# The beginning of a graph kernel: weights loaded ahead of the adjacency, and the start's steps in another order

## The chip, the cores and the metric

The kernel runs on one core of a Trainium2 chip. The core has five engines with an instruction queue each: TensorE (PE, matrix products), VectorE (DVE), ScalarE (ACT), GpSimd (POOL) and SyncE (SP, which here only issues transfers). Each runs its queue in order, and waits on semaphores for the others. The metric is the device time of one execution in microseconds (us), median of several runs. "The profile" is one execution recorded by the hardware profiler. Its own time is given beside its span, the time from its first to its last instruction.

## The reference

128 independent graphs of 128 nodes with 64 features; `adj` is 128 x 128 for each graph, about one entry in eight is positive.

```python
mask = (adj > 0.0)
h  = relu(layernorm(x))
# layer 0: for each edge j-k a hidden row of 192
hid[j,k] = relu(h[j] @ W1a + (h[j] - h[k]) @ W1b + b1)
x1 = x + sum_k(mask[j,k] * hid[j,k]) @ W2 + deg[j] * b2
# layer 1: plain aggregation
out = x1 + (adj @ relu(layernorm(x1))) @ W.T
```

## The kernel before, in words

The graphs are taken in 32 groups of four. For each group the kernel loads `x` and `adj`, normalises `x` into `h`, turns it on TensorE (`hT`), and turns `adj` (`adj_pe`, `adj_act`) to make `maskT`. A product with the weights `wp` gives `pp` (`pp_pe`): for each node its part as the edge's start, its part as the edge's end, and a third block of 64 columns. A second product, a row of ones times `biasp`, adds the bias to `pp`. The projections are then cut into three bf16 parts that add up to the f32 value, called `ca` (`pp_ca`, `pp_rest`, `pp_second`, `pp_third`: first part, what is left, second part, third part). Twelve transfers (`stack`, tile `k`) put these parts under each other so that one matmul sums them.

The edges are found by rank. A product of `maskT` with a triangular matrix counts the edges of each node within each quarter of its neighbours. Comparing these ranks with 0 to 5 gives one-hot rows `S`. In group 0 this is done by `first_ranks` (matmul into `pk`, ScalarE copy to `q`) and `first_slots(0, q)` (six VectorE comparisons for quarter q, four quarters), and in later groups by `rank_pe`, `rank_act` and `slot`. `over` and `count_pe`/`count_dve` count edges beyond six in a quarter, and yield the degrees and the scale `ns` that `pp_z` and the degree column `dn` that `pp_e` need.

The main work of a group is 24 jobs (`Job`). `fill` multiplies `S` and `k` into one of three PSUM buffers `g`; `drain` reduces it on VectorE (tile `hm`, two thirds of the jobs) or on ScalarE and GpSimd (tile `T`). TensorE can fill three jobs ahead; the fourth needs a drained buffer. After the jobs come the second layer and the output.

Before group 0 the weights are prepared. `weight_loads` issues W1 on SyncE's queue and four small loads on ScalarE's. `weights_a` halves W2 (`w2h`) and spreads b1. `weights_b` adds the halves of W1 (`wab`, into `wp`), turns the sum, and copies it to `wT`; `weights_b2` multiplies `wT` by `w2h` into `pc`, copies that to `wp`, and adds `b2s` to the product `pbw` to complete `bias`. `weights_c(i)`, i = 0 to 2, splits `bias` into three bf16 parts, three VectorE steps for each part but the last, which has two: a cast (`bp`), the part's share of `biasp`, and the remainder (`br`).

What sets the order: the class `Engine` (its calls all appear as L198 in the profile) holds VectorE, ScalarE, GpSimd and SyncE to the written order during the beginning and in groups 1 to 30; matmuls (L181) and transposes (L184) always keep the written order. Group 0's jobs and the steps of `PLAN0` beside them are left to the scheduler. Two things outside the written lines matter. A transfer carries one of eight semaphores in turn, so an issue also waits until the transfer eight before it in that count has landed. And `buffer` hands out PSUM buffers in turn (three `g`, two `m`), so a step can wait for the last reader of its buffer. `keep_busy` issues matmuls whose result nobody reads; TensorE has them between group 0's counts and its jobs.

The beginning is written as calls from `load(0)` (L1119) to `Engine.held = False`.

Of the kernel before, what the change touches and what calls it, by code (L numbers as in the profile page):

```python
# [150 lines left out]
def kernel(  # L151
# [28 lines left out]
    def mm(*args, **kw):  # L180
        return tc.keep_in_program_order(nc.tensor.matmul(*args, **kw))  # L181

    def tp(*args, **kw):
        return tc.keep_in_program_order(nc.tensor.transpose(*args, **kw))  # L184
# [43 lines left out]
    with ExitStack() as main:  # L228
# [16 lines left out]
        def gtile(name, key=None):  # L245
            i = buffer("g", key, 3)
            return ps_g.tile([P, 2, 512], F32, tag=f"g{i}", name=name)

        def mtile(name, key=None):
            i = buffer("m", key, 2)  # L250
            return ps_m.tile([P, 512], F32, tag=f"m{i}", name=name)
# [54 lines left out]
        def constants():  # L306
            vec.tensor_scalar(ioe, iov, BIG, None, ALU.add)
            vec.tensor_reduce(
                id32, ident.rearrange("p (q j) -> p j q", q=Q), AX.X, ALU.add
            )  # L310
            vec.tensor_copy(id3, id32)

        def constants2():
            vec.tensor_copy(identb, ident)
            vec.tensor_copy(upb, upper)
# [12 lines left out]
        def weight_loads():  # L328
            act.dma_start(w2a, W2[0:C0, :])
            act.dma_start(b1c, b1[0:C0].unsqueeze(1))  # L330
            act.dma_start(bias[:, 0:H], b1.unsqueeze(0).to_broadcast([P, H]))
            act.dma_start(b2s, b2.unsqueeze(0).to_broadcast([P, O]))
            for p in range(2):
                s = slice(p * F, (p + 1) * F)
                sp.dma_start(w1[s], W1.rearrange("(t f) h -> f t h", t=2))

        def weight_loads2():
            for p in range(2):
                s = slice(p * F, (p + 1) * F)
                sp.dma_start(w2bd[s, p, :], W2[C0:H, :])  # L340
                sp.dma_start(wl1[s, s], W)
# [8 lines left out]
            vec.tensor_copy(b1x, b1c.to_broadcast([P, P]))  # L350

        def weights_b():
            pbw = gtile("pbw")
            mm(pbw[:, 0, 0:O], b1x, w2h, start=True, stop=True)
            vec.tensor_tensor(wab, w1[:, 0], w1[:, 1], ALU.add)
            tp(pbw[:, 1, 0:P], wab[:, 0:C0], ident)
            vec.tensor_scalar(wp[:, 0:H], w1[:, 1], -1.0, None, ALU.mult)
            vec.tensor_copy(wT, pbw[:, 1, 0:P])
            return pbw

        def weights_b2(pbw):
            pc = mtile("pc")
            mm(pc[:, 0:O], wT, w2h, start=True, stop=True)
            vec.tensor_copy(wp[:, 2 * H : 2 * H + O], pc[:, 0:O])
            vec.tensor_tensor(bias[:, H : H + O], pbw[:, 0, 0:O], b2s, ALU.add)

        left = [bias]

        def weights_c(i):
            pt = one.tile([P, H + O], BF16, tag=f"bp{i}", name=f"bp{i}")  # L370
            vec.tensor_copy(pt, left[i])
            if i == 0:
                vec.tensor_scalar(biasp, pt, id64[:, i : i + 1], None, ALU.mult)
            else:
                vec.scalar_tensor_tensor(
                    biasp, pt, id64[:, i : i + 1], biasp, ALU.mult, ALU.add
                )
            if i < 2:
                left.append(one.tile([P, H + O], F32, tag=f"br{i}", name=f"br{i}"))
                vec.tensor_tensor(left[i + 1], left[i], pt, ALU.subtract)  # L380
# [3 lines left out]
            tp(pl[:, 0:P], wl1, ident)  # L384
            vec.tensor_copy(wl1t, pl[:, 0:P])

        groups: dict[int, dict] = {}

        def bc(t, n, axis):
            shape = list(t.shape)  # L390
# [4 lines left out]
        def norm_a(src, u):  # L395
            st = tmp.tile([P, G, 6], F32, tag="st", name=f"st{u}")
            mv = tmp.tile([P, G, 2], F32, tag="mv", name=f"mv{u}")
            for b in range(G):
                vec.bn_stats(st[:, b, :], src[:, b, :])
            for b in range(G):  # L400
                vec.bn_aggr(mv[:, b, :], st[:, b, :])
            return mv
# [36 lines left out]
        def stats_a(g):  # L439
            d = groups[g]  # L440
            d["mv"] = norm_a(d["x"], f"a{g}")
# [22 lines left out]
            d = groups[g]  # L464
            normed(d["h2"][:, b, :], d["x1"], d["scales"], b)

        def load(g):
            d = groups[g] = {}
            d["x"] = loads.tile([P, G, F], F32, tag="x", name=f"x{g}", bufs=3)
            sp.dma_start(d["x"], x[g * G : (g + 1) * G].rearrange("b n f -> n b f"))  # L470
            d["adj"] = loads.tile([P, G, N], F32, tag="adj", name=f"adj{g}")
            sp.dma_start(d["adj"], adj[g * G : (g + 1) * G].rearrange("b j k -> j b k"))

        def keep_busy(tile, n):
            for _ in range(n):
# [2 lines left out]
        def adj_pe(g):  # L478
            d = groups[g]
            pt = d["pt"] = mtile(f"pt{g}", "adj_pe")  # L480
            for b in range(G):
                tp(pt[:, b * N : (b + 1) * N], d["adj"][:, b, :], ident)

        def adj_act(g):
            d = groups[g]
            d["adjT"] = grp.tile([P, G, N], F32, tag="adjT", name=f"adjT{g}", bufs=4)
            act.activation(
                d["adjT"].rearrange("k b j -> k (b j)"), d["pt"], AF.Copy
            )
# [12 lines left out]
        def rank_pe(g):  # L502
            d = groups[g]
            d["pq"] = mtile(f"pq{g}", "rank_pe")
            mm(
                d["pq"], triq, d["maskT"].rearrange("k b j -> k (b j)"), start=True, stop=True
            )
# [28 lines left out]
                        d["S"][q * QN : (q + 1) * QN],  # L536
                    )

        def first_ranks(g, qp):

            d = groups[g]
            pk = gtile(f"pk{g}_{qp}")
            if qp == 0:
                d["q3"] = tmp.tile([K3, Q, G * N], BF16, tag="T", name=f"q3{g}", bufs=3)
            for i in range(2):
                q = 2 * qp + i
                mm(
                    pk[0:K3, i], triq3[:, q].rearrange("k t j -> k (t j)"),
                    d["maskT"].rearrange("k b j -> k (b j)"), start=True, stop=True,
                )  # L550
            act.activation(d["q3"][:, 2 * qp : 2 * qp + 2], pk[0:K3], AF.Copy)

        def first_slots(g, q):

# [8 lines left out]
        def hT_pe(g):  # L563
            d = groups[g]
            ph = d["ph"] = mtile(f"ph{g}", "hT_pe")
            for r in range(2):
                tp(
                    ph[:, r * N : (r + 1) * N],
                    d["h"][:, r].rearrange("n p f -> n (p f)"),
                    ident,  # L570
                )

        def hT_act(g):
            d = groups[g]
            d["hT"] = tmp.tile([P, 2, N], F32, tag="hT", name=f"hT{g}", bufs=1)
            act.activation(
                d["hT"].rearrange("p r n -> p (r n)"), d["ph"][:, 0 : 2 * N], AF.Copy
            )
# [59 lines left out]
        def pp_ca(g, r):  # L638
            act.activation(part(g, r, 0), both(g, r), AF.Copy)
# [35 lines left out]
        def pre_proj(g, r, between=None):  # L675
            pp_pe(g, r, between)
            pp_ca(g, r)
            return (
                lambda: pp_rest(g, r), lambda: pp_z(g, r), lambda: pp_e(g, r),
                lambda: pp_second(g, r), lambda *engines: pp_third(g, r, engines),  # L680
            )
# [434 lines left out]
        ORDERL += c0s[12:]  # L1116


        load(0)  # L1119
        weight_loads()  # L1120
        groups[0]["mv"] = norm_a(groups[0]["x"], "a0")
        constants2()
        groups[0]["scales"] = norm_s(groups[0]["mv"], "a0")
        weights_a()
        constants()
        adj_pe(0)
        pre_norm(0)
        adj_act(0)
        pb = weights_b()
        load(1)  # L1130
        weight_loads2()
        hT_pe(0)
        hT_act(0)
        weights_b2(pb)
        mask(0)
        for i in range(3):
            weights_c(i)
        steps = [pre_proj(0, 0, lambda: first_ranks(0, 0))]
        first_slots(0, 0)
        steps[0][0]()  # L1140
        steps += [pre_proj(0, 1, lambda: (rank_pe(0), rank_act(0), over(0)))]
        (residual, zs, es, second, third), (residual1, zs1, es1, second1, third1) = steps
        residual1()
        count_pe(0)
        count_dve(0)
        second()
        second1()
        third(pool, pool)
        third1(vec, vec)
        stack(0)  # L1150
        first_slots(0, 1)
        adj_pe(1)
        adj_act(1)
        mask(1)
        stats_a(1)
        keep_busy(mtile("keep"), 14)
        zs()
        es()
        zs1()
        es1()  # L1160
        first_ranks(0, 1)
        first_slots(0, 2)
        pre_norm(1)
        first_slots(0, 3)
        Engine.held = False
        ahead = {}

# [62 lines left out]
```

## Time and profile before

| what | us |
|---|---|
| time, median of 3 runs | 922.36 (919.47, 922.36, 926.63) |
| profiled execution, own time | 924.5 |
| its span | 922.7 |
| TensorE busy | 881.8 (96% of the span) |
| VectorE busy | 820.5 (89%) |
| ScalarE busy | 767.4 (83%) |
| GpSimd busy | 721.9 (78%) |
| mean granted TensorE clock | 0.984 of full |
| first job's matmuls start (`g`) | 24.45 |
| first `hm` reduction starts | 28.42 |

The first four rows compare executions: the profiled one lies 2.1 above the median of the three, which spread over 7.2. The busy shares are means over the whole span; TensorE's 96% says which engine limits the long middle, and nothing of the first 60 us, where every engine has gaps. The last two rows are positions in the span and mark where the beginning ends.

### The profile page before, as it was taken

What the parts mean: (1) busy time and instruction counts of PE and PEld (TensorE: products, weight loads), DVE (VectorE), ACT (ScalarE), POOL (GpSimd) and SP (SyncE); (2) the same over time, 40 slices, a digit from 0 to 9 for tenths busy, and PEclk for the clock granted to TensorE, in tenths of its full rate; (3) what the DMA queues carried; (4) which work ended last, traced back from release to release, by engine and by line L of the source; (5) the groups of instructions that cost most, each with busy time, mean ns of one, the idle gap of its engine ahead of it and who ended that gap; (6) DMA issues with size and microseconds to landing.
All of it is one profiled execution on the core that took longest, in us unless ns stands there. A gap on an engine that the chain in (4) does not pass through costs nothing.

```text
span 922.7 us, 26432 instructions
## 1 busy us (share of the span) xinstructions
PE 881.8 (96%) x9721; PEld 679.0 (74%) x9722; DVE 820.5 (89%) x2070; ACT 767.4 (83%) x1722; POOL 721.9 (78%) x1098
## 2 busy tenths in 40 slices
PE   5789999999999999999999999999999999999995
PEld 2467777777777777777777777777777777777774
DVE  6769999999999998899999999999999999999953
ACT  4659888889888888988888988888898888899841
POOL 1368888888888888788888888888888888888873
PEclk9799999999999999999999999999999999999997
DMA  3627666667666666766666766666676666577610
GB/s 91 133 70 160 156 151 141 141 144 178 151 155 149 142 140 157 162 155 154 141 140 141 179 155 152 147 140 141 157 167 155 156 144 138 142 169 162 137 25 15
DMA packets 88294, 129.88 MB, mean 141 GB/s; under 512 B 47200, under 2 KB 63968, under 8 KB 88160
## 3 DMA queue, kind: packets, MB, share of 16 engines
q1 hardware_dynamic: 87584, 127.98, 60.8%
q8 instruction: 78, 1.28, 0.6%
q14 instruction: 56, 0.46, 0.1%
q10 hardware_dynamic: 576, 0.16, 0.1%
HBM read 13.01 MB, written 4.19 MB: 19 GB/s over the span
## 4 chain that ended last, share of the span: by engine, by line
PE 80%; DVE 7%; POOL 5%; ACT 3%; DMA 2%; issue 2%; SPq 1%; DVEq 0%; POOLq 0%; ACTq 0%
PE g L181 45%; PE pp L181 7%; PE px L181 6%; PE pe L181 6%; PE py L181 5%; DVE hm L198 4%; POOL T L198 4%; PE po L181 2%; PE pj L181 2%; PE pt L184 2%; DMA k<-ca 1%; ACT T L198 1%; PE pga L181 1%; DVE S L198 1%; PE pd L181 1%
## 5 line engine op out<-in xcount | busy, mean ns | idle before, releaser
L198 POOL TENSOR_TENSOR T<-T 128x192 f32<-128x192 f32 (+2 forms) x768 | 524.1, 688 | 116.8 <-ACT T L198 72.1
L198 DVE TENSOR_REDUCE hm<-g 128x64 f32<-128x768 f32 x512 | 471.2, 951 | 44.3 <-PE g L181 44.0
L181 PEld LDWEIGHTS <-k 96*128 96x128 bf16 (+1 forms) x5544 | 362.1, 105 | 145.8 <-issue 55.9
L181 PE MATMUL g<-S,k 96*128 96x384 bf16 (+1 forms) x2048 | 373.4, 330 | 20.3 <-DVE hm L198 12.8
L181 PE MATMUL g<-id,k 96*64 96x192 bf16 (+1 forms) x3496 | 308.6, 247 | 0.0
L198 ACT ACTIVATE T<-g 128x768 f32<-128x768 f32 x256 | 197.5, 810 | 105.6 <-PE g L181 96.0
L198 POOL TENSOR_TENSOR ca<-rest,ca 128x384 bf16<-128x384 f32 x126 | 112.4, 912 | 59.4 <-ACT ca L198 44.8
L198 ACT ACTIVATE g<-at 128x768 f32<-128x768 f32 x150 | 120.4, 816 | 2.6 <-DVE hm L198 2.4
L198 DVE TENSOR_SCALAR S<-qs 128x512 bf16<-128x512 bf16 x186 | 88.5, 491 | 0.3 <-ACT qs L198 0.3
L181 PE MATMUL pe<-RT,X 128*64 128x128 f32 (+1 forms) x512 | 70.5, 280 | 0.0
L181 PE MATMUL pp<-wp,hT 64*128 64x448 f32 x256 | 67.5, 604 | 0.4 <-DVE bias L198 0.4
L198 ACT ACTIVATE z<-pp,ns 128x128 f32<-128x128 f32 (+1 forms) x256 | 66.6, 361 | 0.0
L198 DVE TENSOR_TENSOR rest<-pp,ca 128x768 f32<-128x768 f32 x64 | 60.6, 946 | 0.4 <-ACT ca L198 0.4
L198 ACT ACTIVATE h<-x,mra,rsa 128x64 f32<-128x64 f32 x128 | 56.9, 449 | 1.8 <-issue 1.3
L181 PEld LDWEIGHTS pe<-RT,X 128*64 128x64 f32 (+1 forms) x512 | 52.7, 165 | 5.5 <-issue 5.4
L198 ACT ACTIVATE ca<-rest 128x768 bf16<-128x768 f32 x64 | 53.9, 841 | 1.7 <-DVE rest L198 1.7
L181 PE MATMUL px<-ca,S 128*128 128x192 bf16 x384 | 53.2, 248 | 0.8 <-DVE S L198 0.8
L198 ACT ACTIVATE ca<-pp 128x768 bf16<-128x768 f32 x64 | 51.8, 810 | 1.6 <-PE pp L181 1.6
L181 PE MATMUL px<-ca,R 128*128 128x192 bf16 x384 | 53.2, 248 | 0.0
L181 PE MATMUL pe<-ident,z 128*128 128x128 f32 x192 | 49.1, 283 | 0.0
L198 POOL TENSOR_TENSOR hm<-T 128x64 f32<-128x64 f32 x128 | 41.1, 321 | 9.9
L198 ACT ACTIVATE et<-iov,mid 128x128 f32<-128x128 f32 x128 | 47.5, 399 | 0.0
(127 smaller groups left out, 1243.5 us busy)
## 6 DMA issues: line engine op xcount, KB each, us to landing
S<-S SPq DMA_DIRECT2D x372, 192.0 KB, 4.1
k<-ca SPq DMA_DIRECT2D x384, 96.0 KB, 2.2
adj<-in_adj_dram SPq DMA_DIRECT2D x32, 256.0 KB, 3.2
x<-in_x_dram SPq DMA_DIRECT2D x32, 128.0 KB, 2.6
out_dram<-ot SPq DMA_DIRECT2D x32, 128.0 KB, 2.2
w<-in_L_gnn_W_dram SPq DMA_DIRECT2D x2, 96.0 KB, 5.0
bias<-in_L_gnn_b_dram ACTq DMA_DIRECT2D x1, 96.0 KB, 4.1
w2a<-in_L_gnn_W_dram ACTq DMA_DIRECT2D x1, 32.0 KB, 2.2
```

What stands on the lines that cost most here:

```text
L181: return tc.keep_in_program_order(nc.tensor.matmul(*args, **kw))
L184: return tc.keep_in_program_order(nc.tensor.transpose(*args, **kw))
L198: ins = f(*args, **kw)
```

## The change

Only the beginning is rewritten; the jobs and `PLAN` are the same text. The lines that matter:

```diff
-            act.dma_start(bias[:, 0:H], b1.unsqueeze(0).to_broadcast([P, H]))
             act.dma_start(b2s, b2.unsqueeze(0).to_broadcast([P, O]))
+            act.dma_start(bias[:, 0:H], b1.unsqueeze(0).to_broadcast([P, H]))
...
-        load(0)
+        load_x(0)
         weight_loads()
+        load_adj(0)
         groups[0]["mv"] = norm_a(groups[0]["x"], "a0")
-        constants2()
         groups[0]["scales"] = norm_s(groups[0]["mv"], "a0")
         weights_a()
-        constants()
-        adj_pe(0)
         pre_norm(0)
-        adj_act(0)
         pb = weights_b()
         load(1)
         weight_loads2()
+        bias_b2(pb)
+        weights_b1(pb)
+        weights_c(0)
         hT_pe(0)
+        adj_pe(0)
         hT_act(0)
-        weights_b2(pb)
+        adj_act(0)
+        weights_b2()
         mask(0)
-        for i in range(3):
-            weights_c(i)
-        steps = [pre_proj(0, 0, lambda: first_ranks(0, 0))]
-        first_slots(0, 0)
-        steps[0][0]()
-        steps += [pre_proj(0, 1, lambda: (rank_pe(0), rank_act(0), over(0)))]
...
-        count_pe(0)
-        count_dve(0)
-        second()
-        second1()
-        third(pool, pool)
-        third1(vec, vec)
-        stack(0)
-        first_slots(0, 1)
-        adj_pe(1)
-        adj_act(1)
-        mask(1)
-        stats_a(1)
-        keep_busy(mtile("keep"), 14)
-        zs()
-        es()
-        zs1()
-        es1()
-        first_ranks(0, 1)
-        first_slots(0, 2)
-        pre_norm(1)
-        first_slots(0, 3)
+        weights_c(1)
+        weights_c(2)
+        pp_pe(0, 0, lambda: (turns.update(g=2), first_ranks_pe(0, 0)))
+        turns["g"] = 1
+        pp_pe(0, 1)
+        rank_pe(0)
+        pp_ca(0, 0)
+        pp_ca(0, 1)
+        pp_rest(0, 0)
+        pp_rest(0, 1)
+        pp_second(0, 0)
+        pp_second(0, 1)
+        pp_third(0, 0, (pool, pool))
+        pp_third(0, 1, (vec, vec))
+        rank_act(0)
+        first_ranks_act(0, 0)
+        stack(0)
+        over(0)
+        count_pe(0)
+        first_slots(0, 0)
+        count_dve(0)
+        first_slots(0, 1)
+        adj_pe(1)
+        keep_busy(mtile("keep"), 9)
+        for r in range(2):
+            pp_z(0, r)
+            pp_e(0, r)
+        adj_act(1)
+        turns["g"] = 2
+        first_ranks_pe(0, 1)
+        first_ranks_act(0, 1)
+        first_slots(0, 2)
+        mask(1)
+        constants2()
+        constants()
+        stats_a(1)
+        first_slots(0, 3)
+        pre_norm(1)
```

The helpers are cut to fit: `load` is now `load_x` plus `load_adj`; `first_ranks` is split into its matmuls (`first_ranks_pe`) and its ScalarE copy (`first_ranks_act`). `weights_b` ends before the copy to `wT`; `weights_b1` does this copy and the product `pc`, `weights_b2` the copy of `pc` to `wp`, and `bias_b2` the addition of `b2s`. `pbw` now lies in an `m` buffer.

In the built programs the queues of group 0 differ in these places, and nowhere after the first groups: SyncE issues x, W1, W1, adj where it issued x, adj, W1, W1; ScalarE issues b2s before b1's row; the five constant steps stand on VectorE between `first_slots(0, 2)` and `first_slots(0, 3)`, with `mask(1)` and `stats_a(1)`; the scheduler places group 2's layernorm statistics among group 0's jobs instead of ahead of them; TensorE has 9 keep-busy matmuls for 14.

## The prediction

> **What bounds the kernel now.** I read the page's slices first. TensorE is full from the fourth slice (about 70 us) to the end at full clock; no step of the change lies there, so the change can only move the moment at which this middle begins. The slices' columns are 23 us wide.
>
> ```profile
> PE   5789999999999999999999999999999999999995
> DVE  6769999999999998899999999999999999999953
> PEclk9799999999999999999999999999999999999997
> ```
>
> Next the chain that ended last, in order of time, for the first 32 us (start, length, what).
>
> ```profile
> 2.66 5.53 DMA w<-in_L_gnn_W_dram
> ...
> 13.98 1.89 PE pp L181 x6
> 15.87 0.55 PE pq L181
> ...
> 19.20 4.88 PE keep L181 x14
> 24.08 0.55 PE pk L181 x2
> 24.65 1.03 ACT q L198
> 25.71 1.30 DVE S L198 x6
> ```
>
> Three things hold the start: W1's landing at 8.19, the bias's three-part split on VectorE (until 13.93), and the 14 keep-busy matmuls, behind which the second half of the ranks (pk, q, S) queues. VectorE's timeline (start, length, idle before) shows what stands between that and the first job's reduction:
>
> ```profile
> 8.29 0.36 DVE L198 TENSOR_TENSOR wp<-w 128x192 f32<-128x192 f32 x1 [2.38 <-DMA w<-in_L_gnn_W_dram]
> ...
> 18.99 0.15 DVE L198 CAST nb<-pd 128x4 bf16<-128x4 f32 x1
> 19.65 1.58 DVE L198 TENSOR_TENSOR ca<-rest,ca 128x384 bf16<-128x384 f32 x2 [0.51 <-ACT ca L198]
> ...
> 25.71 1.30 DVE L198 TENSOR_SCALAR S<-q 96x512 bf16<-96x512 bf16 x6 [0.60 <-ACT q L198]
> ...
> 28.42 2.68 DVE L198 TENSOR_REDUCE hm<-g 128x64 f32<-128x768 f32 x3
> ```
>
> From 19.65 to 32 VectorE idles 0.6 us: it is the bound there. TensorE has filled three jobs by 26.5 and waits for a drained buffer until 29.42. So I measure the change at the first `hm`, now at 28.42; everything later keeps its order.
>
> **The change, part by part.**
>
> *W1 first.* x's issue ends at 1.27, so the W1 issues (0.76 and 0.62) start at 1.32 and 2.12; the second is 0.54 earlier. Its flight is 5.53 now, x's shortest is 2.6: landing between 4.7 and 7.65. What goes from in front is adj's 256 KB, 1.1 us at the 233 GB/s of the microsecond from 2 to 3: I take 7.65 - 1.1 = 6.5, against 8.19. adj lands at 3.4 to 5.5 after an issue near 2.8, by 8.3, and is wanted after 9.2. The later issues of SyncE's queue shift with the semaphores that they wait for; the next load that anybody needs (adj of group 1) is wanted by TensorE at 17.6 now and at 20.2 then: nothing.
>
> *The bias, split between the weight steps.* W1's landing to the end of the `wT` copy took 1.31 (8.19 to 9.50). The addition of b2s now comes ahead of `wT` (0.13 from start to start), so the split could begin at 6.5 + 1.4 = 7.9 instead of 10.95. But a new wait stands here: b1's row is now ScalarE's fourth load, whose issue waits for x and began at 3.39. The fourth load flew 5.0, this row 4.1: it lands at 7.5 to 8.4; I take 8.0, in the middle. Behind this wait on VectorE stand the copy of `pc` and maskT; adj's transposes reuse the buffer of `pc` and so wait too. Cast, share and remainder (10.95 to 11.90) take 0.95: 8.95; copy of `pc` 9.2; four transposes 1.09 and ScalarE's copy 0.58 with hand-overs: maskT at 11.0. From maskT's start to the end of the split was 3.31 (10.62 to 13.93), less the 0.95 already done: biasp complete at 13.4, against 13.93. So of 2.95 us gained at the first cast 0.55 is left, because adj and its mask now lie in the middle.
>
> *Thirds ahead of the comparisons.* The bias products follow at 13.4. For the second half pq (0.55) no longer stands in the way, nor do the copies of q and qs on ScalarE: its first part `ca` starts at 16.94 - 0.55 - 0.55 - 0.2 = 15.65; `rest` 16.5 to 17.45 (now 17.78 to 18.74). VectorE then waits for ScalarE's second part until 18.4 (17.5 + 0.85), does two thirds (1.5, start to start) until 19.9, `over` 0.2, six comparisons 1.22 and only then the counts, 0.5: `nb` ends at 21.85, against 19.14, **2.7 later**, although the thirds are 1.25 earlier. Those would be worth something if the transfers of `k` were awaited; the first matmul of a job shows no such wait. Six issues of 0.71 that end by 21.4 and land 2.2 later (23.6) stay ahead of the jobs (26).
>
> *Nine keep-busy matmuls for fourteen.* They still wait for `nb`'s read of their buffer. Fourteen took 4.88, part at half clock. Nine at half clock (0.43 each) take 3.85, at full clock 1.9, at the mean seen 3.1; TensorE will have idled for some four us before, so I take 3.5: 21.9 to 25.4. Then pk, 0.55 to 1.09, say 0.7, and q 1.03: `first_slots(0, 2)` starts at 27.2, against 25.71, **1.5 later**. VectorE has had S(0,1) and the four `e` until 24.15 and then stands for 3.0: all it could do is queued behind.
>
> *Late constants.* After those comparisons (1.21) now come maskT of group 1 (0.34), the five constants (0.11 + 0.23 + 0.13 + 0.41 + 0.18 = 1.06, from their rows at 4.20 to 5.91) and the statistics (0.78), then S(0,3) 1.21 and a reciprocal 0.1: `hm` at 27.2 + 4.7 = 31.9, where it is 2.71 now. **2.0 more.** Where the constants stood, VectorE waited 2.38 for W1 and the square root anyway: their removal gains nothing beyond that. Group 2's statistics (0.97), moved among the jobs, fall into VectorE's idle 0.69 and 4.47 at 34 to 46: nothing; without that cover, 1.0.
>
> Sum: 1.5 + 2.0 = 3.5 us later at the first `hm`. **924.5 + 3.5 = 928.0** for an execution like the profiled one, which lies 2.1 above the median; so **926** as a median.
>
> The bounds. Low: bias at 7.5 (-0.5), second projections at full clock (1.0 for 1.73: -0.7), keep-busy at full clock (-1.6), pk 0.55: `hm` at 28.9, +0.5. High: W1 at 7.65 (split at 9.05, +1.05), keep-busy 3.85, pk 1.09: +5.3.
>
> **The clock.** One thing follows that the sum can't fix. The granted clock was half in 19.9 to 23.3, 30.1 to 33.5 and 40.4 to 50.6 (rows by microsecond: length, busy time and count of PE, PEld, DVE, ACT, POOL, then the granted clock, DMA share and GB/s):
>
> ```profile
> 30.00:31.00 1.00, 0.65 (x7) 0.36 (x8) 1.00 (x2) 0.31 (x1) 0.00 (x0) 0.56 0.00 0
> 33.00:34.00 1.00, 1.00 (x13) 0.56 (x13) 1.00 (x4) 1.00 (x5) 0.99 (x1) 0.73 0.00 0
> 40.00:41.00 1.00, 0.00 (x0) 0.00 (x0) 1.00 (x4) 0.08 (x2) 0.00 (x0) 0.68 1.00 258
> 50.00:51.00 1.00, 1.00 (x6) 0.27 (x4) 0.69 (x1) 0.00 (x0) 0.51 (x2) 0.70 0.00 0
> ```
>
> The switches lie inside these four microseconds (granted 0.56, 0.73, 0.68, 0.70), and the stretches are 3.4, 3.4 and 10.2, whole multiples of 3.4. TensorE idle for 2.36 at 38.7 brought the long one, idle for 1.61 at 53.6 brought none. In 30 to 51 it was busy 3.0 and 8.7 us at half clock, which full clock would have done in half: 5.9 us that depend on where a gap falls.
>
> The Trainium skill ("TensorE: Matmul & The Clock Gate", Part 1: The HAM clock gate) says that full clock needs about one fully busy window of 3.4 us, and that the windows run freely, not from the kernel's start. The rows' multiples of 3.4 agree. This speaks against the shorter keep-busy: nine matmuls at half clock fill 3.85 us, which need not contain a whole window, and fourteen would. By the rule pk then takes 1.09 and keep-busy 3.85, and the sum is 0.7 more; by the rows taken above it is as given.
>
> **The rivals.**
>
> *Faster after all: the clock stays full.* The place is the long stretch 40.4 to 50.6. If the 2.4 us gap before it (two `hm`, `e`, `rest`: unchanged work) falls across two windows, so that neither holds over 2 us of idleness (between the 1.61 and the 2.36 above), 8.7 us at half clock become 4.35; with the stretch at 30.1 too, 5.9. That is 926 - 4.4 to - 5.9: 920 to 921.5, faster than before by 1 to 2. For it: the moment is shifted by 3.5, about one window. Against: the gap ahead of the fourth job, now 2.8, grows to four.
>
> *The clock goes lower.* If the gap at 53.6 also trips it, three windows between 50 and 62 run at half clock, each costs about 1.7: 926 + 5 = 931; with a late W1 932.5. For it: more idleness in the start; against: the same work after 40.
>
> *The start loses nothing.* q is ready when VectorE is (keep-busy at full clock), all at the low bounds: +0.5, 923. For it: W1 and bias are earlier; against: counts now behind thirds and comparisons.
>
> **How the numbers follow.** Forecast (923.5 to 928.5) 0.48; clock full 0.18; clock lower 0.2; nothing lost 0.08; something not seen 0.06. The range, 919 to 932, takes in all but the edges of the clock cases. One per cent (9.2 us) is about what a measurement of this kernel can tell from no change: faster than 913.1 needs what I do not see (0.05); slower than 931.6 takes the lower half of the bad clock case and the unseen (0.13); within 1% the rest, 0.82.
>
> **What would show it.** Right: in VectorE's timeline `wp` near 6.5, the first cast of the split near 8.0 behind a transfer, `nb` near 21.8, S from the second q at 27 with some 3 us idle before it, first `hm` near 32. Wrong: `hm` below 30 (then the wait behind keep-busy was mis-sized), a job waiting for `k`, or a changed pattern of half clock between 30 and 60.

## The result and the profile after

The changed kernel took **929.25 us** in the median of 6 runs (927.16 to 931.37); the kernel before, run beside it, 923.36 in the median of 6 (919.47 to 926.63). The ratio is **1.0068 (95%: 1.0041 to 1.0094)**: slower by 5.9 us, which is inside the 1% that the prediction called no change, inside its range, and above its forecast's own band (923.5 to 928.5).

The profiled execution of the changed kernel took 927.16, the shortest of its six, with a span of 925.4; the profiled one of before lies above its median. The two traces therefore differ by only 2.7 us, and show less than half of what the runs show. This decides how the rest has to be read: positions are taken from traces, sizes from the runs.

The slices of the page, changed kernel:

```profile
PE   4789999999999999999999999999999999999995
DVE  6659999999999999999999999999999999899953
PEclk8789999999999999999999999999999999999997
```

As before, TensorE is full from the fourth slice on. The first three lost: 4, 7, 8 for 5, 7, 8 on TensorE, and a granted clock of 8, 7, 8 for 9, 7, 9. So the change cost time in the first 70 us. The granted clock fell there too.

VectorE's timeline, changed kernel (start, length, operation, idle before it and what ended that):

```profile
5.91 0.36 DVE L198 TENSOR_TENSOR wp<-w 128x192 f32<-128x192 f32 x1 [0.65 <-DMA w<-in_L_gnn_W_dram]
...
8.03 0.29 DVE L198 CAST bp<-bias 128x256 bf16<-128x256 f32 x1 [0.71 <-DMA bias<-in_L_gnn_b_dram]
...
10.95 0.43 DVE L198 TENSOR_SCALAR maskT<-adjT 128x512 bf16<-128x512 f32 x1 [1.83 <-ACT adjT L198]
...
20.64 0.15 DVE L198 CAST nb<-pd 128x4 bf16<-128x4 f32 x1
...
25.55 1.30 DVE L198 TENSOR_SCALAR S<-q 96x512 bf16<-96x512 bf16 x6 [2.40 <-ACT q L198]
...
27.90 0.18 DVE L198 CAST id<-id 128x32 bf16<-128x32 f32 x1
...
30.07 0.92 DVE L198 TENSOR_REDUCE hm<-g 128x64 f32<-128x768 f32 x1
```

W1 is used at 5.91 instead of 8.29. The bias then waits for its own row (8.03), and its split has the mask in its middle, so that the bias products on TensorE start at 13.34 instead of 13.98: of 2.4 us gained, 0.64 are left. The thirds ahead of the counts turn this into `nb` 1.65 later (20.64 for 18.99). That is one execution: in the traces of e2, e6 and e9 below, with the same steps up to there, the second projection took 1.72 or 1.73 and not 0.93, and `nb` starts at 21.50 to 21.73. VectorE then stands for 2.40 until the second half of the ranks is copied, and the first `hm` comes at 30.07 for 28.42, again 1.65 later.

TensorE's timeline, changed kernel, shows what VectorE's cannot:

```profile
13.34 0.28 PE L181 MATMUL pp<-biasp,oneb 64*128 64x256 bf16 x2 [0.32 <-DVE biasp L198]
13.45 0.93 PE L181 MATMUL pp<-wp,hT 64*128 64x448 f32 x4
...
19.23 0.19 PE L181 MATMUL pd<-oneb,ov 128*128 128x1 bf16 x1 [4.42 <-DVE ov L198]
...
20.85 3.18 PE L181 MATMUL keep<-oneb 128*128 128x512 bf16 x9 [0.32 <-DVE nb L198]
23.87 0.59 PE L181 MATMUL pk<-maskT,triq 128*96 128x512 bf16 x2
24.30 0.49 PE L181 MATMUL g<-S,k 96*128 96x384 bf16 x2
28.14 0.49 PE L181 MATMUL g<-id,k 96*128 96x192 bf16 x4 [3.35 <-DVE id L198]
...
31.04 0.80 PE L181 MATMUL g<-S,k 96*128 96x384 bf16 x2 [1.07 <-DVE hm L198]
```

The first job multiplies by `S` at 24.30 and then **waits 3.35 us for the constant `id`**, which VectorE finishes at 28.1 because the constants now stand behind `first_slots(0, 2)`. Before, `id` had been ready for 19 us and there was no wait, as VectorE's and TensorE's timelines of that kernel show:

```profile
5.73 0.18 DVE L198 CAST id<-id 128x32 bf16<-128x32 f32 x1
```

```profile
24.45 0.49 PE L181 MATMUL g<-S,k 96*128 96x384 bf16 x2
24.78 0.49 PE L181 MATMUL g<-id,k 96*128 96x192 bf16 x4
```

The fourth job (31.04) then takes 0.80 for two matmuls that took 0.49 in the jobs ahead of it: half clock. The rows by microsecond, changed kernel (length, busy time and count of PE, PEld, DVE, ACT, POOL, then granted clock, DMA share, GB/s), where it switches:

```profile
16.00:17.00 1.00, 0.00 (x0) 0.00 (x0) 0.32 (x1) 0.98 (x2) 0.58 (x1) 0.61 0.40 95
...
23.00:24.00 1.00, 1.00 (x6) 0.54 (x5) 0.15 (x1) 0.13 (x1) 0.00 (x0) 0.98 0.55 132
...
29.00:30.00 1.00, 0.97 (x12) 0.78 (x10) 1.00 (x7) 0.20 (x1) 0.00 (x0) 0.93 0.00 0
30.00:31.00 1.00, 0.00 (x0) 0.00 (x0) 1.00 (x5) 0.00 (x0) 0.00 (x0) 0.50 0.00 0
...
36.00:37.00 1.00, 1.00 (x13) 0.71 (x10) 0.00 (x0) 1.00 (x4) 0.84 (x2) 0.65 0.86 172
...
43.00:44.00 1.00, 0.21 (x2) 0.21 (x4) 0.97 (x5) 0.32 (x1) 0.00 (x0) 0.76 1.03 215
...
53.00:54.00 1.00, 1.00 (x6) 0.15 (x2) 0.37 (x1) 0.00 (x0) 0.24 (x1) 0.62 0.00 0
```

Half clock lasted from 16.2 to 23.0 (6.8 us; before 3.4, from 19.9), from 29.9 to 36.7 (6.8; before 3.4, from 30.1) and from 43.5 to 53.8 (10.2; before 10.2). Into the first stretch falls the end of TensorE's idle time of 4.42, ahead of the counts that now stand behind the thirds. The first `hm` of group 1 starts at 67.39 for 64.48: 2.9 later, of which 1.65 was there at 30 us and 1.3 came after it, where the longer stretch lies. After that the distance stays: the last matmuls start 2.65 later.

### The profile page after: what moved, and what is told of

Its sections match the earlier page's. It is cut to its first block, busy times and chain, and to the rows that moved or that the text cites. A ratio compares the mean times of both kernels' runs of the same rounds, so it can differ in the third digit from the quotient of the medians.

```text
span 925.4 us, 26423 instructions
## 1 busy us (share of the span) xinstructions
PE 880.7 (95%) x9717; PEld 678.2 (73%) x9717; DVE 818.9 (88%) x2070; ACT 767.9 (83%) x1722; POOL 720.4 (78%) x1098
## 4 chain that ended last, share of the span: by engine, by line
PE 85%; DVE 6%; POOL 3%; DMA 2%; ACT 2%; issue 1%; SPq 1%; DVEq 0%; POOLq 0%; ACTq 0%
PE g L181 48%; PE pp L181 7%; PE px L181 7%; PE pe L181 7%; PE py L181 5%; DVE hm L198 4%; POOL T L198 2%; PE po L181 2%; PE pt L184 2%; PE pj L181 2%; PE pga L181 1%; DMA k<-ca 1%; PE pd L181 1%; PE pa L181 1%; PE ph L184 1%
## 5 line engine op out<-in xcount | busy, mean ns | idle before, releaser
L198 ACT ACTIVATE ca<-rest 128x768 bf16<-128x768 f32 x64 | 53.8, 840 | 2.2 <-DVE rest L198 2.1
L198 ACT ACTIVATE et<-et,half 128x128 f32<-128x128 f32 x128 | 47.4, 399 | 0.0
```

The costliest lines, as they stand in the source:

```text
L198: ins = f(*args, **kw)
```

## How time at half clock is counted and priced

Each run comes with its span and its mean granted clock. In the rows the clock is full or half, so a run spent (1 - clock) x 2 x span at half clock: 923 us at 0.984 are 29.5 us. The clock is given to three digits, so one run is known to about 1 us, a mean of many better. Over 98 runs of the kernel before, this time has a mean of 24.1 us; over the changed kernel's 6 it is 35.9. In the 14 traces 9.0 to 12.5 us of it lie at the end, behind 907 us or later, where TensorE runs dry (one gap is 3.38 in the trace of before).

The count has a hole. In every trace the rows give full clock over the first matmuls, but these take about twice what the same ones take later. From TensorE's timeline of the kernel before, and its row:

```profile
10.72 1.86 PE L181 MATMUL pp<-wp,hT 64*128 64x448 f32 x4 [0.41 <-DVE bias L198]
```

```profile
11.00:12.00 1.00, 1.00 (x4) 0.22 (x3) 0.93 (x5) 0.00 (x0) 0.00 (x0) 1.00 0.75 224
```

The same four take 1.02 at 35.95 there. How long this lasts differs: the second projection took 1.73 at 14.15 in that trace and 0.93 at 13.45 in the changed kernel's, and in e10's the 14 keep-busy matmuls from 18.24 took 5.55, 0.40 each, under rows of full clock, where 14 in e9 took 3.19, 0.23 each. By the durations the count is some us too low, and not by the same amount in every execution. Kernels with the same matmuls up to 24 us (e4 and e10 with before; e1, e2 and e9 with the changed one; e12 with e1; e11 with e7) should share the error in the mean. Between kernels whose starts differ, the changed one and before among them, it may differ, and the split into clock and the rest is an estimate.

Within one kernel, the runs with more time at half clock are longer: fitted within each of the 14 kernels of this study, 230 runs together, by **0.30 us per us at half clock** (standard error 0.024; 0.30 for the 98 runs of before alone). That is a correlation; an experiment below (e10) changes the clock and little else. The Trainium skill ("TensorE: Matmul & The Clock Gate", Terms) puts the penalty at the throttled time times one minus the clock's share, 0.5 per us. The runs give less, and TensorE is not busy in all of that time: in the row of 30 us above it is at half clock and 0.00 busy.

With 0.30 the result splits: the means differ by 6.4 us (929.2 and 922.8), 11.8 us more at half clock account for 3.5, and 2.9 remain for the later start and for what the count misses. The table gives all kernels that way ("rest" is the mean less 0.30 x the time at half clock). All ratios are against before on the same chip; its medians there were 922.4 to 923.4, and its row takes all 98 runs together.

| kernel | median us | ratio (95%) | half clock us | rest us | first `hm` in its trace |
|---|---|---|---|---|---|
| before | 922.8 | 1 | 24.1 | 915.6 | 28.42 |
| changed | 929.25 | 1.0068 (1.0041–1.0094) | 35.9 | 918.5 | 30.07 |
| e1 early constants | 925.98 | 1.0041 (1.0025–1.0058) | 30.4 | 917.4 | 29.31 |
| e2 fill the wait | 925.12 | 1.0029 (1.0015–1.0044) | 30.8 | 916.0 | 29.84 |
| e3 loads only | 924.32 | 1.0008 (0.9994–1.0023) | 24.0 | 916.7 | 30.15 |
| e4 late constants in before | 925.25 | 1.0023 (1.0006–1.0040) | 29.4 | 916.5 | 28.43 |
| e5 counts first | 926.92 | 1.0041 (1.0022–1.0060) | 32.8 | 916.9 | 28.54 |
| e6 14 keep-busy | 928.28 | 1.0064 (1.0039–1.0089) | 27.6 | 920.3 | 31.98 |
| e7 = e1 and e5 | 925.47 | 1.0021 (1.0005–1.0038) | 24.5 | 917.3 | 26.58 |
| e8 = e7, comparisons later | 928.26 | 1.0065 (1.0041–1.0090) | 31.8 | 919.1 | 24.83 |
| e9 keep-busy under the constant | 925.08 | 1.0021 (1.0000–1.0041) | 22.5 | 918.8 | 32.20 |
| e10 before, gaps kept busy | **919.39** | **0.9972 (0.9956–0.9989)** | 13.3 | 915.8 | 28.02 |
| e11 = e7, gaps kept busy | 925.49 | 1.0034 (1.0017–1.0052) | 20.2 | 919.7 | 27.28 |
| e12 = e1, gaps kept busy | 922.40 | 1.0005 (0.9991–1.0019) | 16.7 | 917.7 | 30.33 |

One trace is one execution, and some lie far from their kernel's median: e2's is 1.8 above, e3's 1.0 above, e6's 2.4 below, e7's 2.7 below, e9's 3.1 above, e11's 1.6 above.

## The experiments: the late constants

**e1: the constants back where they were, all else as changed.**

```diff
         groups[0]["mv"] = norm_a(groups[0]["x"], "a0")
+        constants2()
...
         weights_a()
+        constants()
...
         first_slots(0, 2)
         mask(1)
-        constants2()
-        constants()
```

> The changed kernel with the five constant steps put back where they were before (two after the layernorm statistics, three after the spread of b1). Theory, the late constants cost twice: VectorE's first hm comes 1.06 earlier, at 29.0 instead of 30.07, and the first job's second half no longer waits 3.35 us for the constant id, so that TensorE has three jobs filled by 26.4, as in the kernel before; together 1 to 3 us off the changed kernel, 926 to 928 as a median. Rival, the wait for the second q alone: only the 1.06 at hm, and the median 928. Rival, the constants are hidden: 929, no change.

It took 925.98, 3.3 less than the changed kernel (2.5 by the ratios). Half clock fell from 35.9 to 30.4 us, worth 1.6, and the rest by 1.1, about what the constants take on VectorE. In its trace no matmul waits for `id`, the wait for the second q is the same (2.36), and `hm` starts at 29.31, 0.76 sooner. So they cost more than their 1.06 on VectorE, and by the count the surplus is clock. One trace doesn't show how: half clock begins at 30.0 here too (to 36.8), inside a longer wait of the fourth job, and only the stretch from 43.6 is shorter (3.4 for 10.2).

```profile
30.29 0.80 PE L181 MATMUL g<-S,k 96*128 96x384 bf16 x2 [3.69 <-DVE hm L198]
```

**e4: the opposite, the late constants alone in the kernel before.**

```diff
-        constants2()
         groups[0]["scales"] = norm_s(groups[0]["mv"], "a0")
         weights_a()
-        constants()
...
         first_slots(0, 2)
+        constants2()
+        constants()
         pre_norm(1)
```

> The kernel before with the five constant steps alone moved, to between the comparisons of the third and the fourth quarter. Theory: hm 1.06 later, at 29.5; the first job waits for the constant id until 28.0, so TensorE idles 3 us more ahead of it; 1 to 3 us slower than before, 924.5 to 926.5. Rival: the steps are hidden elsewhere and the start is bound by TensorE: no change, 923.4.

It took 925.25, ratio 1.0023: 2.1 to 2.4 us more. Its first `hm` starts at 28.43, where it was, but only because W1 came earlier in this execution (first used at 7.41, in the trace of before at 8.29): the comparisons ahead of the constants start at 24.82 for 25.71, and from them to `hm` it is 3.61 for 2.71. VectorE's chain is 0.9 longer. The rest rose by 0.9 too; half clock rose by 5.3 us, worth 1.6. TensorE's timeline of this kernel:

```profile
23.57 0.49 PE L181 MATMUL g<-S,k 96*128 96x384 bf16 x2
27.07 0.80 PE L181 MATMUL g<-id,k 96*128 96x192 bf16 x4 [3.02 <-DVE id L198]
27.67 0.85 PE L181 MATMUL g<-S,k 96*128 96x384 bf16 x2
28.31 0.85 PE L181 MATMUL g<-id,k 96*128 96x192 bf16 x4
```

The same wait appears (3.02), and what follows runs at half clock: 0.85 for the same four matmuls that took 0.49. A position in one trace is good to some 0.9 us here, the distance between the two uses of W1.

**e9: the wait is left, but TensorE is kept busy in it.** In the changed kernel, ahead of the first job:

```diff
         first_slots(0, 3)
         pre_norm(1)
+        keep_busy(mtile("keep2"), 14)
+        turns["m"] -= 1
         Engine.held = False
```

> The changed kernel with 14 more keep-busy matmuls where TensorE waited 3.35 us for the constant id, between the second ranks and the first job; nothing else moves, the first hm stays near 30.07. Theory, part of the loss is TensorE's clock, which falls to half after this wait: time at half clock per execution falls from 36 us on average to 25 to 30, and with 0.27 us of time for each us at half clock (the slope inside the kernels run so far) the median falls by 1.5 to 3, to 926.3 to 927.8. Rival, only the position of hm counts: 929, no change.

It took 925.08, 4.2 less than the changed kernel, with 22.5 us at half clock for 35.9. Work was added, nothing was made earlier, and the time fell: the 13.4 us less at 0.30 make 4.0, nearly all of it. That is more half clock than moving the constants took away (5.5 us in e1), so these matmuls do not undo the late constants' share alone. Its trace is one of its longer executions, its first keep-busy ran wholly at half clock (4.02), and so its `hm` at 32.20 isn't representative.

The late constants are thus a large part of the loss: 2.5 to 3.3 us when taken out of the changed kernel, 2.1 to 2.4 when put into the old. Whether it is the largest the runs don't tell: putting the counts first (e5, below) gives back 2.3 to 2.5, and the intervals overlap.

## The experiments: the loads

**e3: only the order of the loads changed, in the kernel before** (W1 ahead of the adjacency, b2s ahead of b1's row).

```diff
-        load(0)
+        load_x(0)
         weight_loads()
+        load_adj(0)
```

> The kernel before with the new order of the loads alone (W1 ahead of adj, b2 ahead of b1's row). Theory: W1 lands near 5.9 instead of 8.19, but TensorE still turns adj first, which lands near 6.7 now, so the weights' products and the split come 1 to 1.5 us earlier; VectorE is the bound from there to the first hm, which comes 0.5 to 1.5 earlier, near 27.3; median 921.5 to 923. Rival, a transfer that moved is the new wait (b1's row, 7.9; adj): no gain at hm, 923.4.

The time is the same, ratio 1.0008 with an interval that takes in 1; the earlier `hm` that was expected did not come. TensorE's timeline of this kernel:

```profile
8.79 1.09 PE L184 MATMUL pt<-ident,adj 128*128 128x128 f32 x4 [8.79 <-DMA adj<-in_adj_dram]
9.66 0.53 PE L181 MATMUL pbw<-w2h,b1x 128*128 128x64 f32 x2
9.98 0.42 PE L184 MATMUL pbw<-ident,wp 128*128 128x128 f32 x1
```

VectorE used W1 at 5.94, but the adjacency stands first in TensorE's order and landed at 8.79, so W1's transpose, and the copy to `wT` behind it (10.44), came later than before (8.70 for the transpose there). The bias products started at 15.20 for 13.98, and the first `hm` at 30.15 for 28.42, with nothing seen in the runs; the rest in the table is 1.1 above that of before. So loading W1 first could pay only together with a later `adj_pe`, and in the changed kernel, which has both, the mask and b1's row stand in the way. No run has those two alone.

## The experiments: thirds, counts and keep-busy

**e5: the comparison, counts and their matmuls ahead of the second and third parts, as before.**

```diff
         pp_ca(0, 1)
+        rank_act(0)
         pp_rest(0, 0)
         pp_rest(0, 1)
+        over(0)
+        count_pe(0)
         pp_second(0, 0)
         pp_second(0, 1)
+        count_dve(0)
         pp_third(0, 0, (pool, pool))
...
-        rank_act(0)
         first_ranks_act(0, 0)
         stack(0)
-        over(0)
-        count_pe(0)
         first_slots(0, 0)
-        count_dve(0)
```

> The changed kernel with rank copy, over and counts put back ahead of the second and third parts, the comparisons staying behind the thirds; constants late as in the change. Theory, thirds ahead of the counts hold back keep-busy and with it the second q: nb ends near 17.9 (now 20.79), keep-busy starts with it, VectorE no longer waits 2.40 us for the second q, first hm at 27.4 instead of 30.07; median 2 to 3 under the changed kernel, 926 to 927. Rival, the clock decides and not VectorE: hm at 27.4 but the median stays at 928 to 930.

`nb` ended 2.1 earlier than in the changed kernel, the wait for the second q shrank from 2.40 to 0.48, `hm` started at 28.54, 1.5 earlier, and the first job still waited 2.83 for `id`. The median is 926.92: 2.3 less than changed (2.5 by the ratios). The median is as expected, `hm` is not (27.4): the start was mended in part, and the wait for the constants stayed.

**e6: 14 keep-busy matmuls for 9 in the changed kernel.**

```diff
-        keep_busy(mtile("keep"), 9)
+        keep_busy(mtile("keep"), 14)
```

> The changed kernel with 14 keep-busy matmuls instead of 9. Theory, they are a wait on the path of the second q: 5 x 0.35 to 0.43 = 1.8 to 2.1 us more, first hm at 32.0, median 930.5 to 931.5. Rival, they earn their time by keeping the clock full: first jobs at full clock, half-clock stretch after 30 one window shorter, median 927 to 929.

Three lines of VectorE's timeline of this kernel:

```profile
21.50 0.15 DVE L198 CAST nb<-pd 128x4 bf16<-128x4 f32 x1
...
27.46 1.30 DVE L198 TENSOR_SCALAR S<-q 96x512 bf16<-96x512 bf16 x6 [3.44 <-ACT q L198]
...
31.98 0.92 DVE L198 TENSOR_REDUCE hm<-g 128x64 f32<-128x768 f32 x1
```

The wait is 1.04 longer and `hm` 1.9 later, but 0.86 of that is already there at `nb`, ahead of the added matmuls; they add 1.06 (4.24 for 3.18). The time is the same (928.28 for 929.25, and the intervals overlap). By the count, half clock fell by 8.3 us, worth 2.5, as the theory of the clock has it, and 1.8 were lost in the rest, as the theory of the wait has it. That both act and cancel is an estimate: the keep-busy matmuls lie in the part where the count has its hole, and the seven runs fall into two lots (925.9 to 926.8, and 928.3 to 931.8).

**e2: the waiting time filled.** In the changed kernel group 1's mask, the constants and the statistics go ahead of `first_slots(0, 2)`, where VectorE stood for 2.40.

```diff
-        first_slots(0, 2)
         mask(1)
         constants2()
         constants()
         stats_a(1)
+        first_slots(0, 2)
         first_slots(0, 3)
```

> The changed kernel with group 1's mask, the constants and group 1's statistics ahead of the comparisons for the second q instead of behind them, in the 2.40 us in which VectorE waited for that q. Theory, order behind the wait: the 2.18 us of these steps vanish in the wait, hm starts at 27.9 (now 30.07, before 28.42), the constant id is there by 25, and the median comes to the kernel before or a little under it, 921 to 925. Rival, the loss lies in the clock's pattern after 30 us and not in VectorE's order: hm at 27.9, but the median stays at 927 to 930.

It took 925.12, just above the 921 to 925 expected, 4.1 less than changed (3.6 by the ratios), and has the lowest rest of the kernels with the new order. No matmul waits for `id` in its trace, though `hm` there is only 0.23 earlier and not at the expected 27.9: in that execution the second projection and all nine keep-busy matmuls ran at half clock (1.72 for 0.93, 4.02 for 3.18), with the same instructions ahead of them. It still needs 1.0029 of the time before.

**e7: e1 and e5 together.**

```diff
+        constants2()          # where e1 has it
...
+        constants()           # where e1 has it
...
+        rank_act(0)           # and over, count_pe, count_dve as in e5
```

> Constants early as in the first run and counts first as in the fifth, the rest of the change kept. Theory, the two losses add: first hm near 26.5, under the kernel before (28.42), median 921 to 923.5. Rival, TensorE's clock takes the gain back because its idle time ahead of the fourth job stays: 924 to 926.

In its trace `hm` starts at 26.58, **1.84 before** that of the kernel before, and group 1's first `hm` at 61.90, 2.6 before; that execution took 922.75. The median is 925.47, though, and the ratio 1.0021: slower. That is the rival's number, but its counted time at half clock equals that of before (24.5 and 24.1), so the clock, as far as it is counted, doesn't explain it. Its runs lie at 921.8 to 923.9 and at 925.2 to 926.3, with the profiled one in the lower lot. What the upper lot does differently no trace shows. This stays open.

**e8: e7, and the second half of the comparisons behind the second and third job.**

```diff
-            1: "seed|1",
-            2: "load|2 edge_pe|0 ...",
+            1: "seed|1 first_slots|0|2",
+            2: "first_slots|0|3 load|2 edge_pe|0 ...",
...
-        first_slots(0, 2)
-        first_slots(0, 3)
...
+                Engine.held = Engine.planned or (g == 0 and t < 4)
```

> As the seventh, and the comparisons for the third and fourth quarter, which the first six jobs don't read, moved behind the second and the third job's reduction, with VectorE held to the written order there. Theory, VectorE's order sets when the jobs run: first hm near 24, TensorE's idle time ahead of the fourth job shrinks from 3 us to below 1.5, the seventh job is filled 2 us earlier; median 918 to 921, faster than both kernels. Rival, the seventh job waits for the same comparisons as before: 921 to 923.5.

The expectation was missed: 928.26. `hm` starts at 24.83, but a new wait takes its place. From TensorE's and VectorE's timelines of this kernel:

```profile
31.30 0.58 PE L181 MATMUL pj<-trib,ov 128*128 128x128 bf16 x4 [3.66 <-DVE mid L198]
```

```profile
28.64 2.47 DVE L198 TENSOR_SCALAR S<-q 96x512 bf16<-96x512 bf16 x6
...
31.10 0.14 DVE L198 TENSOR_TENSOR mid<-half,pv 128x4 f32<-128x4 f32 x1
```

TensorE stands for 3.66 for `mid`, which is behind these comparisons on VectorE, and six comparisons took 2.47, not 1.30. Why they were slow there was not tried. The clock is half from 28.4, inside this wait, to 42.1.

## The experiments: keeping TensorE busy in the gaps

**e10: the kernel before, with keep-busy matmuls in its two long gaps**, 12 after the steps of the second job (before the wait for the first `hm`) and 8 at the start of the tenth job's steps. The gaps, in TensorE's timeline of the kernel before:

```profile
29.42 0.48 PE L181 MATMUL g<-S,k 96*128 96x384 bf16 x2 [2.81 <-DVE hm L198]
...
41.11 0.85 PE L181 MATMUL g<-S,k 96*64 96x384 bf16 x4 [2.36 <-DVE mid L198]
```

```diff
                 ahead.pop((g, t)).drain()
+                if g == 0 and t == 9:
+                    keep_busy(mtile("keep3"), 8)
+                    turns["m"] -= 1
...
                         STEPS[name](g + off, *args)
+                if g == 0 and t == 1:
+                    keep_busy(mtile("keep2"), 12)
+                    turns["m"] -= 1
```

> The kernel before with 12 keep-busy matmuls after the second job, in the 2.8 us in which TensorE waits for VectorE, and 8 ahead of the tenth job's side steps, in the gap of 2.4 us at 39. Theory of the clock: time at half clock falls from 24 us on average to 12 to 18, median 1.5 to 3.3 lower, 919.7 to 921.5, faster than both. Rival, the added matmuls hold up the jobs behind them or the clock falls in other gaps: 922.5 to 925.

**919.39, ratio 0.9972 (0.9956 to 0.9989): faster than both kernels.** Half clock fell from 24.1 to 13.3 us; 10.8 x 0.30 = 3.2, and the means differ by 3.1 (922.8 and 919.8), so that the rest is that of before (915.8 and 915.6). The price of 0.30 thus holds where the clock is changed on purpose; e9 above (13.4 us and 3.7 in the means) and e12 below (13.7 and 3.8) give 0.28. One thing came along: the scheduler put two layernorm steps of group 2 elsewhere (`mra` at 29.75 for 33.42, one `h` behind `z`). No run has that alone; in e9 and e12 VectorE's order is that of the kernels they come from. TensorE's timeline of this kernel, and its clock:

```profile
25.36 2.75 PE L181 MATMUL keep<-oneb 128*128 128x512 bf16 x12
...
29.02 0.48 PE L181 MATMUL g<-S,k 96*128 96x384 bf16 x2 [0.21 <-DVE hm L198]
...
37.10 1.89 PE L181 MATMUL keep<-oneb 128*128 128x512 bf16 x8
...
39.77 0.52 PE L181 MATMUL g<-S,k 96*64 96x384 bf16 x4 [0.31 <-DVE rest L198]
```

```profile
40.00:41.00 1.00, 1.00 (x17) 0.63 (x13) 0.00 (x0) 1.00 (x4) 0.12 (x1) 1.00 0.85 264
```

The fourth job's idle time is 0.21 where it was 2.81, and the clock is full where it was 0.68 and then half until 50.6. The matmuls fill time that VectorE's `hm` or `rest` takes anyway. The first `hm` of group 1 starts at 59.90, 4.6 earlier than in the trace of before; 0.4 of that was there at the first `hm` (28.02 for 28.42).

**e12 and e11: the same two groups in e1 and in e7.** They ask whether the new start is better once the clock no longer counts.

```diff
+                    keep_busy(mtile("keep3"), 8)     # as in e10
...
+                    keep_busy(mtile("keep2"), 12)    # as in e10
```

> The first run's kernel (the change with its constants early, first hm at 29.3) with the same two added groups of keep-busy matmuls as in the tenth run. Theory, what the change costs without the late constants is its later first hm (0.9) and the clock: half clock near 13 us on average instead of 30.4, median 920 to 922, within 2 us of the tenth run's 919.4. Rival, the new order of the start has a further cost that the clock doesn't explain, as the eleventh run hints: 924 to 926.

> The seventh run's kernel (changed beginning, constants early, counts first, first hm at 26.6) with the same two added groups of keep-busy matmuls. Theory of the clock: half clock falls from 24.5 us on average to 12 to 18, median from 925.5 to 922 to 924. Rival: the seventh run's lost time has another cause than the clock and stays: 925 to 926.

e12 took 922.40 and e11 925.49. Both have less half clock than the kernels that they come from (16.7 for 30.4, 20.2 for 24.5), and both lose to e10: e12, the changed kernel less its late constants and much of its half clock, by 3.0. That lies between the two forecasts. Its first `hm` is 2.3 later than e10's (30.33 for 28.02) and its rest 1.9 higher: the new order without the late constants costs about 2 us that the count of the clock doesn't explain. e11 took the rival's time. In its trace `hm` is earlier (27.28), but TensorE then waits 1.66 for `mid`, behind statistics of group 2 that VectorE ran between the second and third `hm`. In e7 they stand behind the jobs' first four `hm`, so the scheduler changed more than the clock there, and e11 doesn't settle what e7 left open. As in e7, the earlier start isn't found again in the time.

## Why the prediction was right or wrong

- **W1 first:** 6.5 forecast, 5.91 measured, from a flight of 3.7 to 3.9. The new wait at the first cast was right to 0.03 (8.0 and 8.03), the end of the split too (13.4 and 13.3). That little of W1's gain is left in the middle was right.
- **Thirds ahead of the comparisons:** `nb`'s delay was given as 2.7 and is 1.65 in the changed kernel's trace. The second projection ran at full clock there (0.93 for 1.73), which the low bound had as 0.7 us, and the thirds ended at 18.9 where 19.9 was forecast. In the traces of e2, e6 and e9 it ran at half clock, and `nb` came 2.5 to 2.7 later than before, as forecast. The mechanism is as described, and e5 shows it; its size goes by the execution.
- **Nine keep-busy matmuls:** 3.5 forecast, 3.18 measured; the idle time of VectorE before the second q was 2.40 for 3.0. Right. What the prediction set against them, that nine need not contain a whole busy window of those in the Trainium skill ("TensorE: Matmul & The Clock Gate", Part 1: The HAM clock gate), is neither met nor broken by one trace: the clock rose to 0.98 in the row of 23 us in the changed kernel, with the nine running from 20.85, but all nine stayed at half clock in e2 and e9 (4.02). By the count of the runs, fourteen have 8.3 us less of half clock, with the reserve made at e6.
- **The first `hm`:** 31.9 forecast, 30.07 measured: 1.65 later, not 3.5. The prediction named "below 30" as wrong; it is just above, and the wait was mis-sized rather than absent. In e9's trace, with the same steps on VectorE and `nb` and the nine matmuls late, it is 32.20.
- **Late constants: here the prediction failed.** It counted the five constants as 1.06 on VectorE behind the comparisons, and said of the place that they left "their removal gains nothing beyond that". It followed the moved steps on their own queue and didn't ask who reads them: `id` is an operand of the first job. TensorE's wait of 3.35 was in no term, and no rival had it. Undoing this one move gives back 2.5 to 3.3 us: the forecast 1.06 is found again (1.1 in the rest), and the 1.6 beside it is half clock, which the sum had at nothing.
- **The clock:** "One thing follows that the sum can't fix" treated it as a draw around nothing, between a rival at -5.9 and one at +5. It is a systematic loss: 11.8 us more counted in the mean of the runs, an estimated 3.5 us of the 6.4. The rival "the clock goes lower" had the right sign and size in its cause (more idleness in the start) but the wrong place: the stretches that are longer are 16.2 to 23.0 and 29.9 to 36.7, not 50 to 62; the gap that it named (at 53.6 before, 1.60 at 56.6 now) tripped nothing.
- **The number:** the 2.9 in the rest are near the 3.5 forecast for the later start, though the trace shows only 1.65 of them; the clock's 3.5 was left out of the likeliest case. So the time was 929.25 and not 926.
- **The rivals** "the clock stays full" and "the start loses nothing" did not happen. That less half clock in the start is worth about 3 us is shown by e10 (3.1 in the means), by matmuls put in the gaps and not by the change.

About 1.2 of the 2.9 us in the rest is not in the positions of the first `hm` (1.65). `nb` 0.9 to 1.1 later still, as in the traces of e2, e6 and e9, would make up most of it; how many executions are like that is not on record. What keeps e7 and e11 from gaining by their earlier start is not settled either.

## What to carry to other kernels

When a step is moved later, look for the first instruction on any engine that reads what it makes, not only at what it costs on its own queue. A gap of some 3 us on TensorE that another engine forces can still cost time here, by the half clock behind it, so filler matmuls belong inside such gaps (e10), and not ahead of work that they hold up (e6). A change of clock can't be judged by one trace: the mean granted clock of many runs, priced by the runs of one kernel, helps to tell it from a later start, as long as the durations of the matmuls bear the count out.

## What the runs showed of the hardware that was not expected

- The counted time at half clock varies by run with the same instructions: 18.4 us in some runs of the kernel before (920.1 us in the mean), 29.6 in others (924.6).
- Gaps of 2.35 and 2.36 us on TensorE ended at half clock (e9 at 43.9, before at 41.1), a gap of 1.61 did not. Length alone doesn't decide: a gap of 2.34 that ended at 45.2 in e6's trace brought no half clock. With 12 and 8 matmuls in the gaps of before, the clock was full from 27 to 907 us in e10's trace.
- Over the first matmuls of every trace the rows give full clock while the durations are those of half clock: 1.86 or 1.87 for the first projection in all 14, where it takes 1.02 later. Which is right is not shown directly; the durations, which fall by half within the start, speak for half clock.
- The same load lands up to 1.0 us apart between traces: in kernels with the load order of before, W1 is first used at 8.29, 7.41 and 7.33.
